# A ring of three x blocks, loads of two blocks by 4 MB, and products copied straight to the output buffer in a kernel for pairwise feature products

## The chip, the cores and the metric

The kernel runs on one core of a Trainium2 chip. The metric is the device time of one execution in microseconds (us). Each kernel was executed several times; the text gives the median of the fast runs with their lowest and highest value. A ratio is the mean time of one kernel's fast runs over the mean of the other's in the same rounds, so it is not quite the ratio of the two medians.

## The reference

```python
# r_inputs: (4096, 32, 64) float32, W: (496, 64, 64) float32; 496 = 32 * 31 / 2 pairs
idx_i, idx_j = np.triu_indices(F, k=1)
vi = inputs[:, idx_i, :]
vj = inputs[:, idx_j, :]
vidots = jnp.einsum('bpd,pde->bpe', vi, W)
return vidots * vj                      # (4096, 496, 64) float32, 520 MB
```

For every pair of features i < j, the 64 values of feature i are multiplied by a 64 x 64 matrix, and the result is multiplied elementwise by feature j. The result is 520 MB; inputs and weights are 42 MB.

## The kernel before

The batch is cut into 32 tiles of 128 rows, one row per partition; two tiles make a block of x (2 MB). Per tile, TensorE (PE) transposes (turns) x and multiplies it by the turned weights into PSUM, the memory that holds its results; a step is up to 16 pairs. VectorE multiplies the step by feature j into an output buffer. For some steps ScalarE copies the PSUM result to a temporary, and GpSimd multiplies that into the output buffer. A tile has five output groups (90 to 105 pairs, about 3 MB each), and three output buffers rotate. Each full group goes out by one transfer from the SyncE queue.

```python
xpool = ctx.enter_context(tc.tile_pool(name="xpool", bufs=2))   # two blocks of x, a tile each
tpool = ctx.enter_context(tc.tile_pool(name="tpool", bufs=4))   # temporaries, and reordered W
opool = ctx.enter_context(tc.tile_pool(name="opool", bufs=3))   # output groups
...
LATE = 6
loads = {place[blk * NB, LATE]: blk + 1 for blk in range(2, NBLK - 1)}   # one 2 MB load per block
...
        if i in aside and c0 == 0 and s not in no_aside:
            tmp = tpool.tile([P, CH, 2, E2], F32, tag="tmp", name=f"tmp_{s}")
            nc.scalar.copy(tmp, src)
            nc.gpsimd.tensor_mul(dst, tmp, xj)
        else:
            nc.vector.tensor_mul(dst, src, xj)
```

At the start, W comes in four chunks. Each is reordered by copies (`order_w`, into `rp`), then turned by PE. The copies of the last chunk are written at step 54 and 55 of the program.

Of the kernel before, what the change touches and what calls it, by code (L numbers as in the profile page):

```python
# [8 lines left out]
F32 = mybir.dt.float32  # L9
# [3 lines left out]
def kernel(  # L13
# [16 lines left out]
    nc = tc.nc  # L30

    B, F, D = x.shape
    P = 128
    NB = 2
    assert 2 * D == P and B % (NB * P) == 0
    NBLK = B // (NB * P)
    NP = F * (F - 1) // 2
    E2 = D // 2
    BANK = 512
    CH = BANK // E2  # L40
    RUN = 2 * BANK // P
# [7 lines left out]
    aside = (1, 3, 5, 7, 9, 11, 13)  # L49
# [2 lines left out]
    wrows = list(zip(cuts[:-1], cuts[1:]))  # L52

    const = ctx.enter_context(tc.tile_pool(name="const", bufs=1))
    xpool = ctx.enter_context(tc.tile_pool(name="xpool", bufs=2))
    xtpool = ctx.enter_context(tc.tile_pool(name="xtpool", bufs=4))
    tpool = ctx.enter_context(tc.tile_pool(name="tpool", bufs=4))
    opool = ctx.enter_context(tc.tile_pool(name="opool", bufs=3))
    psum = ctx.enter_context(tc.tile_pool(name="psum", bufs=4, space=bass.MemoryType.PSUM))

    ident = const.tile([P, P], F32, tag="ident", name="ident")
    make_identity(nc, ident)

    xs = {}

    def rows_of(dram: bass.AP, blk: int) -> bass.AP:
        return dram[blk * NB * P : (blk + 1) * NB * P]

    def new_x(blk: int):

        xs[blk] = xpool.tile([P, 1 + NB * F, D], F32, tag="xs", name=f"xs_{blk}")
        nc.gpsimd.memset(xs[blk][:, 0, :], 0.0)  # L72

    def load_x(blk: int, eng, k0: int = 0, k1: int = NB):
        src = rows_of(x, blk).rearrange("(p k) f d -> p (k f) d", k=NB)
        eng.dma_start(out=xs[blk][:, 1 + k0 * F : 1 + k1 * F, :], in_=src[:, k0 * F : k1 * F, :])  # L76


    wflat = w.rearrange("p d e -> p (d e)")
# [1 line left out]
    EU = 2 * BANK // P  # L81
    NU = E2 // EU

    def load_w(c: int, eng=nc.sync):

        a, b = wrows[c]
        pool, tag = ((opool, "ot"), (opool, "ot"), (const, "w3"), (const, "w3"))[c]
        raw[c] = pool.tile([P, D * D], F32, tag=tag, name=f"raw_{c}")
        eng.dma_start(out=raw[c][: b - a, :], in_=wflat[a:b])

    def order_w(c: int, k: int, copy):
        r = wrows[c][1] - wrows[c][0]
        rp = tpool.tile([P, EU, 2, D], F32, tag="tmp", name=f"rp_{c}_{k}")
        src = raw[c][:r, :].rearrange("p (d h e) -> p e h d", h=2, d=D)
        copy(rp[:r], src[:, k * EU : (k + 1) * EU])  # L95
        return rp

    def turn_w(c: int, k: int, rp, copy):
        r = wrows[c][1] - wrows[c][0]
        if c not in wT:  # L100
            wT[c] = const.tile([P, r, E2], F32, tag=f"w{c}", name=f"wT_{c}")
        pt = psum.tile([P, EU, P], F32, tag="ps", name=f"ptw_{c}_{k}")
        for n in range(EU):
            nc.tensor.transpose(  # L104
                pt[:, n, :r], rp[:r, n].rearrange("p h d -> p (h d)"), ident[:r, :r]
            )
        copy(wT[c][:, :, k * EU : (k + 1) * EU], pt[:, :, :r].rearrange("p e r -> p r e"))  # L107

    def turn_x(blk: int, k: int, q: int, copy):

        pt = psum.tile([P, RUN, P], F32, tag="ps", name=f"ptx_{blk}_{k}_{q}")
        for n in range(RUN):
            s = k * F + q * RUN + n
            nc.tensor.transpose(  # L114
                pt[:, n, :], xs[blk][:, s : s + 2, :].rearrange("p f d -> p (f d)"), ident
            )
        xT = xtpool.tile([P, RUN, P], F32, tag="xT", name=f"xT_{blk}_{k}_{q}")
        copy(xT, pt)  # L118
        return xT
# [16 lines left out]
    LEAD = 3  # L136
# [5 lines left out]
    place = {ts: n for n, ts in enumerate(sched)}  # L142
# [8 lines left out]
    for c, orders, turns in (  # L151
# [4 lines left out]
        for k in range(NU):  # L156
            due.setdefault(orders[k], []).append(("order", c, k))
            due.setdefault(turns[k], []).append(("turn", c, k))
    no_aside = range(52, 67)
    LATE = 6  # L160
    loads = {place[blk * NB, LATE]: blk + 1 for blk in range(2, NBLK - 1)}
    loads[place[LEAD, LATE]] = 2

    new_x(0)
    load_x(0, nc.sync, 0, 1)
    load_w(0)
    load_w(1)
    load_x(0, nc.sync, 1, NB)
    load_w(2)
    new_x(1)  # L170
    load_x(1, nc.sync)

    v, p, a = nc.vector.tensor_copy, nc.gpsimd.tensor_copy, nc.scalar.copy
    xT, rps = {}, {}
    xT[0, 0, 0] = turn_x(0, 0, 0, a)
    due[0] = [d for d in due[0] if d != ("x", 0, 0, 0)]
    for k, copy in enumerate((v, v, v, a)):
        rps[0, k] = order_w(0, k, copy)
# [4 lines left out]
    for s, (t, st) in enumerate(sched):  # L183
        blk, kt = divmod(t, NB)
        g, i, c0, m = steps[st]
        if s in loads:
            new_x(loads[s])
            load_x(loads[s], nc.scalar)
        for what, *args in due.get(s, ()):
            if what == "x":  # L190
                xT[tuple(args)] = turn_x(*args, a)
            elif what == "turn":
                turn_w(*args, rps.pop(tuple(args)), a)
            else:
                c, k = args
                rps[c, k] = order_w(c, k, (v, v, p, v)[c] if k % 2 == 0 else (v, v, p, a)[c])
                if (c, k) == (2, NU - 1):
                    load_w(3, nc.scalar)

        base, end = groups[g]  # L200
        pa = p0[i] + c0
        if pa == base:
            ots[t] = opool.tile([P, cap, D], F32, tag="ot", name=f"ot_{t}_{g}")
        ot = ots[t]
        ps = psum.tile([P, 2, CH, E2], F32, tag="ps", name=f"ps_{s}")
        for c, (lo, hi) in enumerate(wrows):
            lo, hi = max(pa, lo), min(pa + m, hi)
            if lo < hi:
                for h in range(2):
                    n = i + 1 - h  # L210
                    nc.tensor.matmul(  # L211
                        ps[:, h, lo - pa : hi - pa, :],
                        xT[blk, kt, n // RUN][h * D : (h + 1) * D, n % RUN, :],
                        wT[c][h * D : (h + 1) * D, lo - wrows[c][0] : hi - wrows[c][0], :],
                        start=True,
                        stop=True,
                    )
        o = pa - base
        j = 1 + kt * F + i + 1 + c0
        dst = ot[:, o : o + m, :].rearrange("p m (h e) -> p m h e", h=2)  # L220
        src = ps[:, :, :m, :].rearrange("p h m e -> p m h e")
        xj = xs[blk][:, j : j + m, :].rearrange("p m (h e) -> p m h e", h=2)
        if i in aside and c0 == 0 and s not in no_aside:
            tmp = tpool.tile([P, CH, 2, E2], F32, tag="tmp", name=f"tmp_{s}")
            nc.scalar.copy(tmp, src)  # L225
            nc.gpsimd.tensor_mul(dst, tmp, xj)  # L226
        else:
            nc.vector.tensor_mul(dst, src, xj)  # L228

        ends = (p0[2], end) if s < NS and (t, g) == (0, 0) else (end,)  # L230
        if pa + m in ends:
            n0 = p0[2] if len(ends) > 1 and pa + m == end else base
            nc.sync.dma_start(  # L233
                out=rows_of(out, blk).rearrange("(p k) n d -> p k n d", k=NB)[:, kt, n0 : pa + m, :],
                in_=ot[:, n0 - base : pa + m - base, :],
            )
# [27 lines left out]
```

## Time and profile before

| | before |
|---|---|
| time, median (lowest to highest) | 1354.63 us (1353.6 to 1355.21, 4 runs beside the changed kernel) |
| span of the profiled run | 1353.3 us |
| busy: PE, VectorE, GpSimd, ScalarE | 87%, 71%, 39%, 28% |
| rate of HBM (the chip's main memory) over the span | 415 GB/s |
| output transfers / loads of x in the steady part | 160 of about 3 MB / 14 of 2 MB |

The lines that the prediction quotes are not shown again. Two more lines of the same page belong to them: the clock of PE and the bytes moved, in 40 equal slices of the span (one digit, or one number in GB/s, each). They are flat, apart from the start and the end: no place in the kernel moves fewer bytes than its neighbours, and the clock hardly dips (0.948 over the span). With the transfers holding the DMA engines for 98% of the span, I read this as the transfers setting the pace everywhere.

```profile
PEclk9989999989999898999989999899998999989997
...
GB/s 386 370 426 408 424 427 431 428 432 431 418 414 419 433 412 418 422 413 426 428 407 422 417 425 410 423 421 407 425 410 426 419 422 427 401 432 428 415 417 319
```

### The profile page before, as it was taken

The page shows a single profiled execution, that of the slowest core. Times are in us where ns is not written, and L with a number is a line of the kernel's source. Part 1 is how long each engine was busy: PE and PEld are TensorE (multiplying, and loading weights), DVE is VectorE, ACT ScalarE, POOL GpSimd, SP SyncE. Part 2 cuts the span into 40 slices and gives each one's busy share as a digit, 9 for nine tenths or more (in the row PEclk, how much of TensorE's full clock was granted, in tenths as well). Part 3 has the DMA queues.
Part 4 walks back from the last instruction along what each step waited for, and adds up shares of the span by engine and source line. Part 5 has one row for each costly group of instructions (what it writes and reads, how often), then busy time and mean ns, then how long its engine had stood idle before and what let it go on. Part 6 is the DMA issues. An engine that isn't in the chain of part 4 may idle for free.

```text
span 1353.3 us, 17856 instructions
## 1 busy us (share of the span) xinstructions
PE 1180.3 (87%) x7424; PEld 690.9 (51%) x7424; DVE 956.9 (71%) x1262; ACT 374.1 (28%) x367; POOL 530.2 (39%) x246
## 2 busy tenths in 40 slices
PE   6989889889799897988879989888987989988994
PEld 4556545545455454555445545454554545545552
DVE  5778768767677676776757777676775767767774
ACT  3432222222232232222222222222222222223221
POOL 1813424444243443433444334433434434344431
PEclk9989999989999898999989999899998999989997
DMA  9999999999999999999999999999999999999997
GB/s 386 370 426 408 424 427 431 428 432 431 418 414 419 433 412 418 422 413 426 428 407 422 417 425 410 423 421 407 425 410 426 419 422 427 401 432 428 415 417 319
DMA packets 26273, 562.92 MB, mean 416 GB/s; under 512 B 2912, under 2 KB 2912, under 8 KB 3040
## 3 DMA queue, kind: packets, MB, share of 16 engines
q1 hardware_dynamic: 24048, 530.59, 92.4%
q10 hardware_dynamic: 2144, 31.20, 5.5%
q8 instruction: 58, 0.95, 0.3%
q14 instruction: 23, 0.19, 0.0%
HBM read 41.68 MB, written 520.09 MB: 415 GB/s over the span
## 4 chain that ended last, share of the span: by engine, by line
DMA 50%; PE 25%; DVE 17%; POOL 3%; issue 2%; ACT 0%; DVEq 0%; SPq 0%; POOLq 0%; ACTq 0%
DMA out_dram<-ot 50%; PE ps L211 20%; DVE ot L228 17%; PE ptx L114 4%; POOL ot L226 3%; PE ptw L104 1%; DMA raw<-in_L_rec_W_dram 1%; ACT tmp L225 0%; DVE rp L95 0%; POOL rp L95 0%; DVEq L228 0%; ACT wT L107 0%; SPq L76 0%; POOLq L226 0%; SPq L233 0%
## 5 line engine op out<-in xcount | busy, mean ns | idle before, releaser
L228 DVE TENSOR_TENSOR ot<-ps,xs 128x1024 f32<-128x1024 f32 (+15 forms) x1252 | 945.6, 808 | 364.7 <-DMA out_dram<-ot 185.9
L211 PE MATMUL ps<-wT,xT 64*128 64x512 f32 (+13 forms) x6272 | 1034.9, 473 | 132.8 <-DVE ot L228 121.3
L211 PEld LDWEIGHTS ps<-wT,xT 64*128 64x128 f32 x6272 | 563.7, 197 | 569.9 <-DVE ot L228 306.8
L226 POOL TENSOR_TENSOR ot<-tmp,xs 128x1024 f32<-128x1024 f32 x220 | 519.6, 2362 | 647.4 <-ACT tmp L225 457.1
L225 ACT COPY tmp<-ps 128x1024 f32<-128x1024 f32 x220 | 222.7, 1012 | 500.1 <-PE ps L211 459.6
L118 ACT COPY xT<-ptx 128x1024 f32<-128x1024 f32 x128 | 129.6, 1012 | 428.2 <-PE ptx L114 428.2
L114 PE MATMUL ptx<-ident,xs 128*128 128x128 f32 x1024 | 141.2, 281 | 18.5 <-DVE ot L228 9.9
L114 PEld LDWEIGHTS ptx<-ident,xs 128*128 128x128 f32 x1024 | 111.0, 142 | 64.3 <-issue 44.1
L72 POOL MEMSET xs<- 128x64 f32 x16 | 2.4, 152 | 148.6 <-DVE ot L228 148.6
L104 PE MATMUL ptw<-ident,rp 128*128 128x128 f32 (+1 forms) x128 | 19.2, 305 | 3.9 <-DVE rp L95 3.9
L104 PEld LDWEIGHTS ptw<-ident,rp 128*128 128x128 f32 (+1 forms) x128 | 16.2, 160 | 10.3 <-DVE rp L95 5.0
L107 ACT COPY wT<-ptw 128x1024 f32<-128x1024 f32 (+1 forms) x15 | 14.8, 984 | 21.4 <-PE ptw L104 21.4
L95 DVE COPY rp<-raw 128x1024 f32<-128x1024 f32 (+1 forms) x9 | 10.7, 1219 | 11.1 <-DMA raw<-in_L_rec_W_dram 11.1
L95 POOL COPY rp<-raw 128x1024 f32<-128x1024 f32 x4 | 8.0, 1994 | 0.1
L95 ACT COPY rp<-raw 112x1024 f32<-112x1024 f32 (+1 forms) x3 | 5.9, 1959 | 5.1 <-POOL ot L226 3.3
L107 DVE COPY wT<-ptw 128x1024 f32<-128x1024 f32 x1 | 1.2, 1224 | 3.3 <-PE ptw L104 3.3
L118 ACT ACT_TABLE_LOAD x1 | 1.3, 1283 | 0.7 <-PEq L251 0.7
masks.py:197 POOL MEMSET ident<- 128x128 f32 x1 | 0.2, 206 | 0.3 <-POOLq L251 0.3
masks.py:199 POOL TENSOR_SCALAR_AFFINE_SELECT ident<-ident 128x128 f32<-128x128 f32 x1 | 0.3, 295 | 0.0
L251 POOL MEMSET const-float32-0.0<- 128x1 f32 x1 | 0.1, 99 | 0.2 <-issue 0.2
L251 POOL MEMSET const-bfloat16-1.0<- 128x1 bf16 x1 | 0.1, 102 | 0.0
L251 POOL MEMSET const-uint8-127<- 128x1 uint8 x1 | 0.1, 102 | 0.0
(1 smaller groups left out, 0.1 us busy)
## 6 DMA issues: line engine op xcount, KB each, us to landing
out_dram<-ot SPq DMA_DIRECT2D x64, 3360.0 KB, 16.2
out_dram<-ot SPq DMA_DIRECT2D x32, 3168.0 KB, 15.4
out_dram<-ot SPq DMA_DIRECT2D x32, 3104.0 KB, 17.0
out_dram<-ot SPq DMA_DIRECT2D x31, 2880.0 KB, 16.4
xs<-in_r_inputs_dram ACTq DMA_DIRECT2D x14, 2048.0 KB, 16.6
raw<-in_L_rec_W_dram SPq DMA_DIRECT2D x3, 2048.0 KB, 14.3
xs<-in_r_inputs_dram SPq DMA_DIRECT2D x2, 1024.0 KB, 10.9
xs<-in_r_inputs_dram SPq DMA_DIRECT2D x1, 2048.0 KB, 24.6
```

Source lines behind the costliest of these rows:

```text
L72: nc.gpsimd.memset(xs[blk][:, 0, :], 0.0)
L95: copy(rp[:r], src[:, k * EU : (k + 1) * EU])
L104: nc.tensor.transpose(pt[:, n, :r], rp[:r, n].rearrange("p h d -> p (h d)"), ident[:r, :r])
L107: copy(wT[c][:, :, k * EU : (k + 1) * EU], pt[:, :, :r].rearrange("p e r -> p r e"))
L114: nc.tensor.transpose(pt[:, n, :], xs[blk][:, s : s + 2, :].rearrange("p f d -> p (f d)"), ident)
L118: copy(xT, pt)
L211: nc.tensor.matmul(ps[:, h, lo - pa : hi - pa, :], xT[blk, kt, n // RUN][h * D : (h + 1) * D, n % RUN, :], wT[c][h * D : (h + 1) * D, lo - ...
L225: nc.scalar.copy(tmp, src)
L226: nc.gpsimd.tensor_mul(dst, tmp, xj)
L228: nc.vector.tensor_mul(dst, src, xj)
L251: nc = _bacc.Bacc("TRN2", target_bir_lowering=False, num_devices=1)
```

## The change

The intent: fewer and larger loads, no temporary between ScalarE and GpSimd, no repeated zeroing of a guard column. x lives in one array of three slots. A load brings two blocks of x by one 4 MB transfer. ScalarE copies its product to the output buffer, and GpSimd multiplies it there in place. The reordered W uses a part of the third slot that x does not need yet.

```diff
-    xpool = ctx.enter_context(tc.tile_pool(name="xpool", bufs=2))
-    tpool = ctx.enter_context(tc.tile_pool(name="tpool", bufs=4))
 ...
+    NX = 3
+    xs = const.tile([P, 1 + NX * NB * F, D], F32, tag="xs", name="xs")
+    nc.gpsimd.memset(xs[:, 0, :], 0.0)
+
+    def slot(blk: int, k: int, i: int = 0) -> int:
+        b = blk % 2 * (1 + blk // 2 % 2)
+        return 1 + (b * NB + k) * F + i
 ...
+    def load_two(blk: int, eng):
+        n = NB * F
+        dst = xs[:, 1:, :].rearrange("p (b n) d -> p b (n d)", n=n)
+        step = (slot(blk + 1, 0) - slot(blk, 0)) // n
+        src = x[blk * NB * P : (blk + 2) * NB * P].rearrange("(b p k) f d -> p b (k f d)", b=2, k=NB)
+        eng.dma_start(out=dst[:, 0 : step + 1 : step, :], in_=src)
 ...
-        rp = tpool.tile([P, EU, 2, D], F32, tag="tmp", name=f"rp_{c}_{k}")
+        rp = xs[:, 1 + (NX - 1) * NB * F :, :].rearrange("p (n e h) d -> p n e h d", e=EU, h=2)[:, k]
 ...
-    no_aside = range(52, 67)
 ...
-    loads = {place[blk * NB, LATE]: blk + 1 for blk in range(2, NBLK - 1)}
-    loads[place[LEAD, LATE]] = 2
+    loads = {place[LEAD, LATE]: 2}
+    for blk in range(3, NBLK - 1, 2):
+        loads[place[blk * NB, LATE]] = blk + 1
 ...
-        if i in aside and c0 == 0 and s not in no_aside:
-            tmp = tpool.tile([P, CH, 2, E2], F32, tag="tmp", name=f"tmp_{s}")
-            nc.scalar.copy(tmp, src)
-            nc.gpsimd.tensor_mul(dst, tmp, xj)
+        if i in aside and c0 == 0:
+            nc.scalar.copy(dst, src)
+            nc.gpsimd.tensor_mul(dst, dst, xj)
```

By `slot`, even blocks always lie in slot 0 and odd blocks in slots 1 and 2 in turn. So a pair goes to slots 0 and 1, or to slots 0 and 2, and in the second case block 1 (5, 9, 13), at work in slot 1, lies between.

More of the change, by code (lines that the diff above doesn't have):

```diff
@@ L62 @@
     make_identity(nc, ident)
-    xs = {}
+    NX = 3
[4 more added lines that the diff above has]
+        return 1 + (b * NB + k) * F + i
     def rows_of(dram: bass.AP, blk: int) -> bass.AP:
         return dram[blk * NB * P : (blk + 1) * NB * P]
-    def new_x(blk: int):
-        xs[blk] = xpool.tile([P, 1 + NB * F, D], F32, tag="xs", name=f"xs_{blk}")
-        nc.gpsimd.memset(xs[blk][:, 0, :], 0.0)
     def load_x(blk: int, eng, k0: int = 0, k1: int = NB):
         src = rows_of(x, blk).rearrange("(p k) f d -> p (k f) d", k=NB)
-        eng.dma_start(out=xs[blk][:, 1 + k0 * F : 1 + k1 * F, :], in_=src[:, k0 * F : k1 * F, :])
+        eng.dma_start(
+            out=xs[:, slot(blk, k0) : slot(blk, k1 - 1) + F, :], in_=src[:, k0 * F : k1 * F, :]
+        )
+    def load_two(blk: int, eng):
[4 more added lines that the diff above has]
+        eng.dma_start(out=dst[:, 0 : step + 1 : step, :], in_=src)
     wflat = w.rearrange("p d e -> p (d e)")
@@ L112, in turn_x @@
         for n in range(RUN):
-            s = k * F + q * RUN + n
+            s = slot(blk, k, q * RUN + n) - 1
             nc.tensor.transpose(
-                pt[:, n, :], xs[blk][:, s : s + 2, :].rearrange("p f d -> p (f d)"), ident
+                pt[:, n, :], xs[:, s : s + 2, :].rearrange("p f d -> p (f d)"), ident
             )
@@ L158 @@
             due.setdefault(turns[k], []).append(("turn", c, k))
-    no_aside = range(52, 67)
     LATE = 6
-    loads = {place[blk * NB, LATE]: blk + 1 for blk in range(2, NBLK - 1)}
-    loads[place[LEAD, LATE]] = 2
-    new_x(0)
+    loads = {place[LEAD, LATE]: 2}
+    for blk in range(3, NBLK - 1, 2):
+        loads[place[blk * NB, LATE]] = blk + 1
     load_x(0, nc.sync, 0, 1)
@@ L169 @@
     load_w(2)
-    new_x(1)
     load_x(1, nc.sync)
@@ L186 @@
         if s in loads:
-            new_x(loads[s])
-            load_x(loads[s], nc.scalar)
+            load_two(loads[s], nc.scalar)
         for what, *args in due.get(s, ()):
@@ L218 @@
         o = pa - base
-        j = 1 + kt * F + i + 1 + c0
+        j = slot(blk, kt, i + 1 + c0)
         dst = ot[:, o : o + m, :].rearrange("p m (h e) -> p m h e", h=2)
         src = ps[:, :, :m, :].rearrange("p h m e -> p m h e")
-        xj = xs[blk][:, j : j + m, :].rearrange("p m (h e) -> p m h e", h=2)
-        if i in aside and c0 == 0 and s not in no_aside:
-            tmp = tpool.tile([P, CH, 2, E2], F32, tag="tmp", name=f"tmp_{s}")
-            nc.scalar.copy(tmp, src)
-            nc.gpsimd.tensor_mul(dst, tmp, xj)
+        xj = xs[:, j : j + m, :].rearrange("p m (h e) -> p m h e", h=2)
+        if i in aside and c0 == 0:
+            nc.scalar.copy(dst, src)
+            nc.gpsimd.tensor_mul(dst, dst, xj)
         else:
```

## The prediction

> **What bounds the kernel now.** I read the page first: the slices, the DMA queues and the chain of waits.
>
> ```profile
> DMA  9999999999999999999999999999999999999997
> ...
> q1 hardware_dynamic: 24048, 530.59, 92.4%
> q10 hardware_dynamic: 2144, 31.20, 5.5%
> q8 instruction: 58, 0.95, 0.3%
> ...
> HBM read 41.68 MB, written 520.09 MB: 415 GB/s over the span
> ...
> DMA 50%; PE 25%; DVE 17%; POOL 3%; issue 2%; ACT 0%; DVEq 0%; SPq 0%; POOLq 0%; ACTq 0%
> ```
>
> The transfers hold the 16 DMA engines for 98% of the span, while the busiest engine that computes, PE, stands at 87%. The totals of waits say the same: VectorE and GpSimd stop because an output buffer is still on its way to HBM.
>
> ```profile
> DVE ot L228 <- DMA out_dram<-ot: 185.9, 84, 5.8
> ...
> POOL ot L226 <- DMA out_dram<-ot: 153.1, 59, 5.5
> ...
> POOL xs L72 <- DVE ot L228: 148.6, 14, 18.3
> ...
> ACT tmp L225 <- POOL ot L226: 36.1, 9, 5.0
> ```
>
> I then went to the single packets of the trace. A packet of an output row (26880 bytes, one partition) takes 0.996 us, one of 23040 bytes 0.855 us, one of 16384 bytes of x 0.611 us. One engine's sixteenth of all data adds up to about 1304 us. The last completion lands at 1351.6 us. The rest is the q8 line[...]. If they fall to one engine, (1351.6 - 1304) / 58 = 0.8 us each. The completion marks fit this: between the first and the last engine to finish one output transfer lie 2 us at 190 us and, away from loads, 6 to 7 us from 450 us on. So the end is set by one DMA engine that never idles: after 120 us, each output transfer is issued at least 3.7 us, and from 210 us on at least 6.7 us, before the previous one has fully landed. The kernel can only become faster by some idle time in the first 125 us, and only slower if the output queue runs dry.
>
> [...] 16 x 26880 / 0.996 = 432 GB/s. [...] a 2 MB load is 8 packets per engine; taken in turn with 8 output packets it needs 8 x (0.611 + 0.996) = 12.9 us, and with about 2 us to start and finish on the first engine, more on the last, that is the 16.6 us of the issues below (count, size, us to landing). [...] after 4.7 us without work the stretch of 40 matmuls took 7.99 us, after 2.1 us 7.04. [...]
>
> ```profile
> 700.64 7.99 PE ps L211 x40
> ...
> 739.61 7.04 PE ps L211 x40
> ```
>
> ```profile
> xs<-in_r_inputs_dram ACTq DMA_DIRECT2D x14, 2048.0 KB, 16.6
> ```
>
> **The change, part by part.** (1) 15 of 16 memsets of 152 ns go: 2.3 us of GpSimd, beside other work; worth 0. GpSimd's 148.6 us of waiting before them delays nothing that sets the end.
>
> (2) The products go to the output buffer directly. ScalarE loses its wait for a free temporary (36.1 us), but now waits for the landing of the output buffer, which GpSimd waited for anyway (153.1 us). The 1012 ns copy then falls after the landing instead of ahead of it. The group's end is later by at most about 1 us, inside a lead of 6.7 us: worth 0. The exception that kept steps 52 to 66 on VectorE goes too; those lie at about 70 to 95 us. Idle DMA time after the start is 2.5 us in 25 to 50 us, 0.8 in 50 to 75 and 1.6 in 100 to 125 (mean over the engines). I count -1 us.
>
> (3) Seven loads of 4 MB replace 14 of 2 MB. The bytes and packets are the same. A fixed cost saved is beside the transfers: worth 0.
>
> (4) What decides it is in the program order of the changed kernel. The ring puts blocks 4 and 5 (8 and 9, 12 and 13) into slots 0 and 1, which are neighbours, but blocks 2 and 3 (6 and 7, 10 and 11, 14 and 15) into slots 0 and 2, with a step of two over slot 1, in which the block at work lies. For these four loads the build takes the whole stretch as written. Each waits for the products of the first output group (90 pairs) of the tile at work, and the next product on VectorE and on GpSimd, which read slot 1, wait for the load. The three contiguous loads have neither wait. So four times nothing is multiplied from the load's issue to its landing, while the output queue empties.
>
> What one such stall costs the slowest DMA engine, in steady state, from the moment L at which the load is issued and the 90-pair transfer goes out:
> - Work queued at L: before a tile's last output goes out, 7.5 us are left of the previous one (the lead at such an issue where no load is near). 6.3 us later (679.29 to 685.61 in the issue times) 1.2 us of that are left, then 8 x 0.996 = 8.0 and 8 x 0.855 = 6.8: 16.0 us.
> - The load: 16 packets x 0.611 = 9.8 us, and one instruction fetch, 0.8 us. Taken in turn, both queues end together, at L + 26.6. It lands 0.5 us later.
> - From landing to the next output: the same group after a wait in the kernel before:
>
> ```profile
> 689.29 3.83 DVE L228 TENSOR_TENSOR ot<-ps,xs 128x768 f32<-128x768 f32 x4 [3.74 <-DMA out_dram<-ot]
> ...
> 692.62 2.35 POOL L226 TENSOR_TENSOR ot<-tmp,xs 128x1024 f32<-128x1024 f32 x1 [0.97 <-ACT tmp L225]
> ```
>
> The landing was at 689.17, the output was issued at 695.00: 5.8 us, of which the line shows the chain: a product frees a PSUM buffer, PE fills it, ScalarE copies, GpSimd multiplies. After more than 20 us without work PE is at half clock; I choose 0.5 us for it.
> - From issue to running packets: 0.85 us, twice seen where the queue was nearly dry (at 35.83 and 103.63 us).
>
> Idle: 0.5 + 5.8 + 0.5 + 0.85 = 7.7 us. Afterwards the outputs come at intervals of about 7.8, 8.3, 6.5, 7.0 us against transfers of 7.5, 8.0, 8.0, 6.8 plus the fetches, so the queue is near empty for a tile; I choose 0.3 us for gaps. That makes 8 us. In the first of the four, at about 150 us, the queue is shorter (about 11 us) and drains before the load ends too: also 8. Four stalls: 32 us. Sum: 1354.8 + 32 - 1 = 1386 us, 2.3% more.
>
> **The rivals.** (a) The outputs queued cover the stalls: within 2%. For it speaks that each load shares the engines with outputs, so neither runs dry early; against it that the three outputs in the ring are all that is queued, and 16.0 us is no more than what passes during 16 load packets. Each microsecond more in the queue at L takes one off each stall: with 2 more, 1378. (b) All is hidden, DMA is the bound and its bytes are the same: 1354. That would need the load not to wait for the group at work: issued 6.3 us earlier it would leave 6.3 us more behind it, and the cost would be near 1 us each. The waits in the program speak against it. (c) ScalarE, now tied to the output buffers, or GpSimd becomes the bound: GpSimd is busy 39%, ScalarE 28%; even 1 us for each of 160 outputs disappears in the lead. If it did not, I would see some 1400 us or more. (d) The start gains from removed temporaries: at most the 4.9 us of idle above, so 1350 without the stalls.
>
> **Range and chances.** 1381.9 us is the 2% border, 4 us below my number. Stalls of 5 to 10 us give 1374 to 1394. Slower by over 2%: 0.66; within 2%: 0.33; faster: 0.01.
>
> **What would show it.** In the changed profile: four waits of VectorE for the load of x, each of 20 to 27 us, near 155, 435, 770 and 1110 us; in the slices DMA share and GB/s falling in four places and nowhere else; 4 MB loads landing in 24 to 29 us; the chain of waits passing through the load of x for some 7%; q8 still 58 packets; GpSimd's product still 2.36 us in place. It is wrong if VectorE's waits for the load are short, if the queue never dries, or if output transfers are issued late outside these four places.

## The result, and the profile after

The changed kernel took 1396.83 us (1395.98 to 1396.99, 4 runs) against 1354.63: ratio 1.0311, 95% interval 1.0293 to 1.0329. It is slower, as predicted, but by 42 us in place of 31, and outside of the range (1374 to 1394).

The page of the changed kernel, the lines that answer to those of the prediction and of the section above: clock, DMA share and GB/s by slices, the queues (q1 carries the output, q10 the loads that ScalarE issues, q8 instructions), HBM, and the chain by engine and by line.

```profile
PEclk9899889989999699998999969999899988999997
DMA  9899979999999699999999969999999996999997
GB/s 379 320 412 429 409 317 426 429 418 430 431 422 422 248 430 427 428 423 426 431 428 422 410 266 428 429 429 418 431 430 421 419 407 261 427 430 428 429 431 339
...
q1 hardware_dynamic: 24048, 530.59, 89.6%
q10 hardware_dynamic: 2032, 31.20, 5.3%
q8 instruction: 58, 0.95, 0.2%
...
HBM read 41.68 MB, written 520.09 MB: 403 GB/s over the span
...
DMA 54%; PE 23%; DVE 16%; POOL 2%; issue 2%; ACT 2%; DVEq 0%; SPq 0%; ACTq 0%; POOLq 0%
DMA out_dram<-ot 45%; PE ps L219 18%; DVE ot L235 16%; DMA xs<-in_r_inputs_dram 7%; PE ptx L125 4%; POOL ot L233 2%; DMA raw<-in_L_rec_W_dram 2%; ACT ot L232 1%; PE ptw L115 1%; POOL xs L106 1%; ACT xT L129 0%; DVE xs L106 0%; DVEq L235 0%;
```

The bytes are those of before. The GB/s fall to 317, 248, 266 and 261 in four slices, and the clock of PE falls with them, to 0.6 in the second and third and 0.8 in the last; one more dip (320) is in the second slice, which the prediction had not expected to be deeper than before (370). The load of x has entered the chain with 7% of the span.

The totals of waits (total us, times, longest) and the issues of the loads (count, size, median us to landing, that is, to the last completion mark):

```profile
ACT ot L232 <- DMA out_dram<-ot: 271.4, 67, 8.0
...
POOL ot L233 <- DMA xs<-in_r_inputs_dram: 101.4, 4, 26.3
DVE ot L235 <- DMA xs<-in_r_inputs_dram: 99.7, 4, 25.9
DVE xs L106 <- DMA raw<-in_L_rec_W_dram: 19.8, 2, 11.2
```

```profile
xs<-in_r_inputs_dram ACTq DMA_DIRECT2D x7, 4096.0 KB, 25.7
```

Four waits of VectorE and GpSimd for a load of x are new, 25 us each on the mean. The waits for a landed output, which before belonged to GpSimd, now belong to ScalarE. The last of the four lines is the second surprise: VectorE waits twice for a chunk of W, and in the kernel before once (11.1 us).

**One stall.** The load was issued at 452.77 us and landed at 478.45. The windows around it; the columns are the stretch and its length, each engine's busy time and count of instructions, granted clock, DMA share, GB/s:

```profile
core 0: us, PE busy (x) PEld busy (x) DVE busy (x) ACT busy (x) POOL busy (x), PEclk, DMA share, GB/s
453.00:465.00 12.00, 2.09 (x18) 1.29 (x14) 0.00 (x0) 2.02 (x2) 0.00 (x0) 0.72 1.01 406
465.00:478.50 13.50, 0.00 (x0) 0.00 (x0) 0.00 (x0) 0.00 (x0) 0.00 (x0) 0.50 0.59 248
478.50:486.00 7.50, 6.41 (x20) 3.29 (x22) 5.23 (x6) 1.01 (x1) 4.71 (x2) 0.52 0.00 0
486.00:495.00 9.00, 9.00 (x70) 5.58 (x66) 6.73 (x10) 4.05 (x4) 7.09 (x3) 1.00 0.96 406
```

First the engines stand and the transfers go on; then the engines work and nothing is transferred. In the third row 0 GB/s are moved while PE works at a mean granted clock of 0.52. The timeline of the restart (start, length, engine, tile, idle time before it and what ended that):

```profile
478.57 2.89 DVE L235 TENSOR_TENSOR ot<-ps,xs 128x768 f32<-128x768 f32 x3 [25.89 <-DMA xs<-in_r_inputs_dram]
...
479.59 8.88 PE L219 MATMUL ps<-wT,xT 64*128 64x512 f32 x34 [23.44 <-DVE ot L235]
...
481.71 1.01 ACT L232 COPY ot<-ps 128x1024 f32<-128x1024 f32 x1 [24.46 <-PE ps L219]
...
482.80 2.35 POOL L233 TENSOR_TENSOR ot<-ot,xs 128x1024 f32<-128x1024 f32 x1 [1.83 <-ACT ot L232]
...
484.48 1.89 DVE L235 TENSOR_TENSOR ot<-ps,xs 128x1024 f32<-128x1024 f32 x2 [0.88 <-PE ps L219]
485.77 0.33 SPq L240 DMA_DIRECT2D out_dram<-ot  x1
```

The same group in the kernel before, after a wait of 3.7 us:

```profile
690.30 5.69 PE L211 MATMUL ps<-wT,xT 64*128 64x512 f32 x28 [2.42 <-DVE ot L228]
...
691.53 1.01 ACT L225 COPY tmp<-ps 128x1024 f32<-128x1024 f32 x1 [2.60 <-PE ps L211]
...
695.00 0.33 SPq L233 DMA_DIRECT2D out_dram<-ot  x1
```

From VectorE's first product (478.57, before 689.29) ScalarE's copy starts after 3.14 us in place of 2.24, and the output is issued after 7.20 us in place of 5.71. Before, GpSimd's product came last (end at 694.97). After, it is VectorE's, which waited 0.88 us for PE.

**The start.** Windows of 50 to 62 us, first after, then before:

```profile
50.00:62.00 12.00, 5.30 (x16) 3.08 (x18) 4.91 (x5) 2.87 (x2) 0.53 (x1) 0.59 0.63 259
```

```profile
50.00:62.00 12.00, 12.00 (x80) 7.32 (x78) 8.25 (x9) 6.20 (x7) 10.85 (x5) 1.00 0.99 361
```

VectorE's timeline there says why, in the changed kernel:

```profile
44.84 0.96 DVE L235 TENSOR_TENSOR ot<-ps,xs 128x768 f32<-128x768 f32 x1 [1.19 <-POOL ot L233]
54.39 1.03 DVE L106 COPY xs<-raw 112x1024 f32<-112x1024 f32 x1 [8.60 <-DMA raw<-in_L_rec_W_dram]
```

The copy that reorders the last chunk of W (112 rows) stands among the products of the first tile's second output group and waits 8.60 us for its chunk. In the trace it is the 25th instruction that VectorE executes; in that of the kernel before it is the 47th, at 75.64 us. PE, whose PSUM buffers VectorE does not free, stands too (busy for 5.30 of the 12 us), and no output is ready.

**Where the 42 us lie.** I lined up the same output transfers of the two runs by the time of their last landing, at places where both kernels had loaded equally much. The changed kernel is later by 15.2 us after the first stall, 24.5 after the second, 33.6 after the third and 42.2 after the fourth, and by nothing more from there on. So stalls two to four cost 9.3, 9.1 and 8.6 us, and the start with the first stall 15.2.

### The profile page after: what moved, and what is told of

It is laid out like the page before. It is cut to its first block, busy times and chain, and to the rows that moved or that the text cites. A ratio compares the mean times of both kernels' runs of the same rounds, so it can differ in the third digit from the quotient of the medians.

```text
span 1395.1 us, 17912 instructions
## 1 busy us (share of the span) xinstructions
PE 1145.0 (82%) x7424; PEld 673.5 (48%) x7424; DVE 948.2 (68%) x1258; ACT 377.8 (27%) x371; POOL 537.9 (39%) x235
## 4 chain that ended last, share of the span: by engine, by line
DMA 54%; PE 23%; DVE 16%; POOL 2%; issue 2%; ACT 2%; DVEq 0%; SPq 0%; ACTq 0%; POOLq 0%
DMA out_dram<-ot 45%; PE ps L219 18%; DVE ot L235 16%; DMA xs<-in_r_inputs_dram 7%; PE ptx L125 4%; POOL ot L233 2%; DMA raw<-in_L_rec_W_dram 2%; ACT ot L232 1%; PE ptw L115 1%; POOL xs L106 1%; ACT xT L129 0%; DVE xs L106 0%; DVEq L235 0%; SPq L78 0%; SPq L240 0%
## 5 line engine op out<-in xcount | busy, mean ns | idle before, releaser
L219 PE MATMUL ps<-wT,xT 64*128 64x512 f32 (+13 forms) x6272 | 995.6, 460 | 160.6 <-DVE ot L235 148.9
L233 POOL TENSOR_TENSOR ot<-ot,xs 128x1024 f32<-128x1024 f32 x224 | 529.3, 2363 | 828.6 <-ACT ot L232 711.8
L219 PEld LDWEIGHTS ps<-wT,xT 64*128 64x128 f32 x6272 | 544.4, 190 | 576.7 <-DVE ot L235 301.6
L232 ACT COPY ot<-ps 128x1024 f32<-128x1024 f32 x224 | 226.9, 1013 | 579.0 <-PE ps L219 301.7
L115 PE MATMUL ptw<-ident,xs 128*128 128x128 f32 (+1 forms) x128 | 20.0, 315 | 13.0 <-DVE ot L235 9.1
L115 PEld LDWEIGHTS ptw<-ident,xs 128*128 128x128 f32 (+1 forms) x128 | 16.9, 165 | 19.2 <-issue 14.2
L106 DVE COPY xs<-raw 128x1024 f32<-128x1024 f32 (+1 forms) x9 | 9.1, 1042 | 19.8 <-DMA raw<-in_L_rec_W_dram 19.8
L106 POOL COPY xs<-raw 128x1024 f32<-128x1024 f32 x4 | 8.0, 2022 | 1.6 <-PE ptw L115 1.6
L106 ACT COPY xs<-raw 112x1024 f32<-112x1024 f32 (+1 forms) x3 | 6.0, 1988 | 1.8 <-DMA raw<-in_L_rec_W_dram 1.8
## 6 DMA issues: line engine op xcount, KB each, us to landing
out_dram<-ot SPq DMA_DIRECT2D x32, 3168.0 KB, 16.5
xs<-in_r_inputs_dram ACTq DMA_DIRECT2D x7, 4096.0 KB, 25.7
```

The source lines that it names most:

```text
L106: copy(rp[:r], src[:, k * EU : (k + 1) * EU])
L115: nc.tensor.transpose(pt[:, n, :r], rp[:r, n].rearrange("p h d -> p (h d)"), ident[:r, :r])
L219: nc.tensor.matmul(ps[:, h, lo - pa : hi - pa, :], xT[blk, kt, n // RUN][h * D : (h + 1) * D, n % RUN, :], wT[c][h * D : (h + 1) * D, lo - ...
L232: nc.scalar.copy(dst, src)
L233: nc.gpsimd.tensor_mul(dst, dst, xj)
```

## The experiments

The theory after reading the traces: two causes, the four loads that step over a slot in use (9 us each, 36 together) and the moved copies of W at the start (6 us). Rivals: that 4 MB loads, or the copy straight to the output buffer, cost something by themselves.

**e1_two_loads**, each pair of blocks by two loads of 2 MB, so that no load steps over a slot:

```diff
-            load_two(loads[s], nc.scalar)
+            load_x(loads[s], nc.scalar)
+            load_x(loads[s] + 1, nc.scalar)
```

> The changed kernel with each 4 MB load made as two 2 MB loads, one for each slot, so that no load steps over the slot at work. Theory (the step over the slot at work makes products and load wait for each other, four times about 9 us; the rest, about 6 us, is lost at the start): 1396.8 - 36 = 1361 us, no wait of VectorE for a load of x after the start, four dips of the DMA share gone. Rival (the ring itself, or ScalarE's copy to the output buffer, costs something at every output): the time stays above 1380.

Measured: 1361.05 us (1360.1 to 1362.52), ratio 1.0051 (1.0036 to 1.0066). 35.8 of the 42.2 us are gone with the stepping loads, and VectorE and GpSimd no longer wait for any load of x (nor do they in e2).

**e2_middle_slot**, the loads stay at 4 MB, but even blocks lie in the middle slot, so that both kinds of pair are neighbours (one more zero column, and blocks 0 and 1 of four swap their place in memory):

```diff
-        b = blk % 2 * (1 + blk // 2 % 2)
-        return 1 + (b * NB + k) * F + i
+        b = (1, 0, 1, 2)[blk % 4]
+        return 1 + (b > 0) + b * SL + k * F + i
+    def dram_block(blk: int) -> int:
+        return blk + (1, -1, 0, 0)[blk % 4]
```

> One 4 MB load for two blocks is kept, but even blocks take the middle slot, so that each pair fills two neighbouring slots and the slot at work is never stepped over. Theory: as e1, 1361 us. Rival (a load of 4 MB itself holds up the outputs for too long, 26 us against 16): stays near 1390, while e1 is fast.

Measured: 1363.33 us (1362.19 to 1364.09), ratio 1.0066 (1.0051 to 1.0081). The dips in the middle have gone, with 4 MB loads; the one at the start (the second digit) is left:

```profile
DMA  9899999999999999999999999999999999999997
```

So it is the step, not the size of the load. The 2.3 us above e1 may be a small cost of the larger loads or of the other layout; these runs do not tell which (e5 below lies 2.7 us above e4 in the same way).

**e3_w_in_place**, the copies of the last chunk of W are held at their place in the program:

```diff
-        copy(rp[:r], src[:, k * EU : (k + 1) * EU])
+        ins = copy(rp[:r], src[:, k * EU : (k + 1) * EU])
+        if c == 3:
+            tc.keep_in_program_order(ins)
```

> The changed kernel, with the copies that reorder the fourth chunk of W held at their place in the program, so that VectorE does not sit in one of them for 8.6 us at 46 us while that chunk is still loading. Theory: 6 us less, 1391 us, the four dips stay, the output that was issued at 62.0 us goes out at about 51. Rival (the start lost its time to ScalarE's copies, which now wait for output buffers): stays at 1397.

Measured: 1390.54 us (1389.32 to 1391.34), ratio 1.027 (1.0253 to 1.0287). 6.3 us come back: the start. The output that went out at 62.0 us in the changed kernel goes out at 49.7.

**e4_both**, e1 and e3 together:

> e1 and e3 together. Theory: the two costs add up and nothing else is left: 1355 us, the same as before. Rival (a further cost of the direct copy or of the ring): 1360 or more remains.

Measured: 1355.81 us (1355.49 to 1356.06), ratio 1.0012 (0.9997 to 1.0026). The two causes add up, and with both removed the kernel before and the changed one take the same time.

**e8_direct_only**, the kernel before with nothing but the direct copy:

```diff
-            tmp = tpool.tile([P, CH, 2, E2], F32, tag="tmp", name=f"tmp_{s}")
-            nc.scalar.copy(tmp, src)
-            nc.gpsimd.tensor_mul(dst, tmp, xj)
+            nc.scalar.copy(dst, src)
+            nc.gpsimd.tensor_mul(dst, dst, xj)
```

> The kernel before with one part of the change alone: ScalarE copies to the output buffer and GpSimd multiplies there; two blocks of x, 2 MB loads, the exception for the steps 52 to 66 and the temporaries for W stay. The build moves VectorE's copy of the fourth chunk of W forward here too. Theory: only the start is lost, 1354.6 + 6 = 1361 us, no waits for x. Rival (the copy's wait for the output buffer costs at every output): 1370 or more, spread over the whole span. Rival (the direct copy gains at the start): below 1353.

Measured: 1360.17 us (1359.25 to 1360.58), ratio 1.0042 (1.0027 to 1.0057). The direct copy, the main part of what the prediction had counted as a gain of 1 us, costs 5.6 (the exception for steps 52 to 66 is still in place here).

**e12_direct_w_in_place**, e8 with the copies of W held as in e3:

> The kernel before with the direct copy into the output buffer alone, and the reordering copies of the fourth chunk of W held at their place in the program. The direct copy alone cost 5.6 us (1360.2); its trace shows VectorE waiting 8.6 us for that chunk, as in the changed kernel. If the moved copies are all of it, the time is that of the kernel before, 1353.5 to 1356 us; if the later copy of ScalarE costs something in steady state, it stays at 1358 to 1361 us.

Measured: 1354.95 us (1354.67 to 1355.14), ratio 1.0 (0.9983 to 1.0017). VectorE's waits for chunks of W, in e8 and in e12:

```profile
DVE rp L95 <- DMA raw<-in_L_rec_W_dram: 19.3, 2, 10.8
```

```profile
DVE rp L95 <- DMA raw<-in_L_rec_W_dram: 11.3, 1, 11.3
```

The direct copy itself costs nothing that these runs can tell; the prediction's account, that ScalarE's later copy fits in the lead of the output queue, agrees with this. The whole cost of e8 was that, with the temporaries no longer used for products, the W copies moved forward in VectorE's order (the first is its 25th instruction in e8 too, and its 51st in e12).

**e6_half_strided**, the stepping loads carry half of each row (2 MB, 8 KB per partition and block); the other half follows 14 steps later by two contiguous loads:

```diff
+            dst = xs[:, 1:, :].rearrange("p (b n) d -> p b n d", n=n)[:, 0:3:2, :F, :]...
+            eng.dma_start(out=dst, in_=src[:, :, 0, :])
...
+            for b in (late, late + 1):
+                tc.keep_in_program_order(load_x(b, nc.scalar, 1, NB))
```

> The changed kernel, but the four strided loads carry only half the rows (2 MB); the other half comes 14 steps later by contiguous loads. VectorE still waits for each strided load, for about 14 to 16 us in place of 25. If what a stall costs is the time in which the output queue is empty: 16.0 us are queued, 8 packets of each queue are taken in turn, so some 6 to 7 us of outputs are left at the landing against 7 to 8 us until the next output runs: at most 1 to 2 us each, 1396.8 - 4 x 7.5 = about 1367 (1361 to 1370). If it is the time in which nothing is multiplied: half the cost stays, about 1379.

Measured: 1398.55 us (1397.7 to 1398.82), ratio 1.0325 (1.031 to 1.034). A miss: half the bytes, and nothing saved. The load did land sooner (20.8 us against 25.6), but the output queue ended sooner with it. The packets of the changed kernel show how the two share an engine. At the end of the stall at 478 us one engine is still at work (start to end in us, size in bytes, queue; q10 is x, q1 output):

```
474.46 - 475.31  23040  q1
475.31 - 475.92  16384  q10
475.92 - 476.77  23040  q1
476.77 - 477.38  16384  q10
477.38 - 477.99  16384  q10
```

In these lines the two queues change after one packet, be it of 23040 bytes (0.85 us) or of 16384 (0.61 us), as long as output is left. An engine has 16 packets of the load. Of output, 184 packets ended between the issue and the landing, 11.5 for each of 16 engines; the engine that is late had some 16 (an estimate: 25.2 us from the issue to its last packet, less 16 x 0.61 us for the load, at 0.95 us each). There both end together, whether the load's packets are of 16 KB or of 8 KB: in the changed kernel and in e6 no output is left at the landing (table below). e6 had halved the packets' size and kept their number. What is left of a stall is the bare restart: the time from the end of both queues to the next output packet.

**e9_half_rows**, **e10_every_2nd_row**, **e11_every_4th_row**: fewer packets instead. The stepping load carries the lower 64 partitions, every second or every fourth partition alone; the others follow 14 steps later.

```diff
-        eng.dma_start(out=dst[:, 0 : step + 1 : step, :], in_=src)
+        r = P // step                                                    # e9: 64 for the stepping loads
+        eng.dma_start(out=dst[:r, 0 : step + 1 : step, :], in_=src[:r])
+        r = 2 if step > 1 else 1                                         # e10 (e11: 4)
+        eng.dma_start(out=dst[::r, 0 : step + 1 : step, :], in_=src[::r])
```

> As the changed kernel, but the four strided loads carry the rows of 64 partitions alone (2 MB, 8 packets of 16 KB for each DMA engine); the rows of the other 64 follow 14 steps later in two contiguous loads of 1 MB. The run that halved the strided load by halving each packet (2 MB, 16 packets of 8 KB) saved nothing: its stalls were as dear as before. Theory, formed from that miss: load and output queue are served packet by packet in turn, the output queue holds some 16 packets per engine when the load is issued, so 16 load packets end with the last output packet whatever their size, and the restart of 8 to 9 us is bare idle time; 8 load packets end when 8 output packets (about 7 us) are left, which cover most of the restart. Then the load lands in some 14 to 17 us in place of 25.7, stalls two to four cost 0 to 3 us each in place of 9, the first, with a shorter queue, 2 to 5, and with the 6 us of the start the time is 1364 to 1374 us. Rival: the cost of a stall is the wait as such, whatever the load's packets: 1390 to 1398 us.

Measured: 1408.84 us (1407.88 to 1409.79), ratio 1.0399 (1.0384 to 1.0415). A miss again, and for another reason, which e10 shows.

> As the run before it with half the rows, but the strided loads carry every second partition (64 of 128) in place of the lower 64; the others follow 14 steps later. In that run the load also had 8 packets per engine and the bare idle time in a stall did fall (slowest engine: from 8.6 us to 4.9 us by the packets in flight), but every packet that ran beside a 64-partition load was slower (16 KB took 0.74 to 0.78 us on the mean in place of 0.58, 313 GB/s during the load in place of 420), which cost more than was saved. If it is the lower half of the partitions that makes packets slow, here they keep their pace: load lands 16 to 18 us after its issue, some 4 to 6 us of output are left then, each stall costs 3 to 5 us in place of 9, time 1372 to 1386 us. If any load of 64 partitions is slow: 1400 to 1410. If the stall costs the same whatever the packets: 1394 to 1398.

Measured: 1387.55 us (1386.44 to 1389.13), ratio 1.0246 (1.0228 to 1.0263), 1.6 us above the stretch given.

> Every fourth partition in the strided loads: 1 MB, 4 packets of 16 KB per engine; the other three quarters follow 14 steps later as six contiguous loads of 0.5 MB. By packets in turn the load lands 11 to 13 us after its issue with 8 us or more of output left, which cover the restart: stalls two to four cost 0 to 2 us, the first 0 to 4, time 1361 to 1370 us if packets keep their pace. If the stall costs the same whatever the packets: 1394 to 1398. If loads of few partitions slow all packets: above 1390 with little idle time, to be told by packet times.

Measured: 1380.32 us (1379.05 to 1381.94), ratio 1.0189 (1.0174 to 1.0204; whether that is over 2% is unclear). 10 us above the stretch given.

The waits of VectorE for the load, in e10 and in e11:

```profile
DVE ot L241 <- DMA xs<-in_r_inputs_dram: 67.2, 4, 16.9
```

```profile
DVE ot L241 <- DMA xs<-in_r_inputs_dram: 50.7, 4, 12.8
```

From the packets of the five traces, for stalls two to four. "Left" is the output still queued at the landing, to its last packet's end; "restart" runs from the last packet of x to the first packet of the next output; "bare" is the time without any packet of data:

| kernel | load, packets per engine | landed after | left | restart | bare |
|---|---|---|---|---|---|
| changed | 16 of 16 KB | 25.6 to 25.7 us | 0 | 8.3 to 8.7 us | 8.3 to 8.7 us |
| e6 | 16 of 8 KB | 20.8 to 20.9 | 0 | 8.2 to 8.6 | 8.2 to 8.6 |
| e9 | 8 of 16 KB | 19.1 to 19.6 | 2.9 to 3.3 | 8.0 to 9.2 | 4.3 to 5.1 |
| e10 | 8 of 16 KB | 16.6 | 3.8 | 8.3 to 9.3 | 3.8 to 4.4 |
| e11 | 4 of 16 KB | 12.4 to 12.5 | 5.5 to 5.6 | 8.9 to 9.4 | 2.1 to 2.5 |

The restart hardly differs among the five. What a stall costs is the restart less what is left in the queue when the load lands, and that depends on the number of the load's packets. In the first stall the queue is shorter, and little was saved: 8.1 us bare in the changed kernel, 8.6 in e10 and 7.0 in e11. e10 should have saved (8.5 - 4.2) x 3 = 13 us by this and saved 9; e11 (8.5 - 2.3) x 3 + 1.1 = 20 and saved 16.5; e6 should have saved nothing and lost 1.7. The 2 to 4 us that are missing I put down to the split itself, with its later small loads; this was not tested. For e11, 8 us or more of output had been expected to be left at the landing, and 5.5 were; the load's first packet ran 4.7 us after its issue (in the changed kernel 3.6 to 3.7).

e9 and e10 have the same packets and bytes. Windows of 10 us within the second stall, while the load runs, e9 first:

```profile
464.00:474.00 10.00, 0.00 (x0) 0.00 (x0) 0.00 (x0) 0.00 (x0) 0.00 (x0) 0.50 1.04 344
```

```profile
456.00:466.00 10.00, 0.00 (x0) 0.00 (x0) 0.00 (x0) 0.00 (x0) 0.00 (x0) 0.50 0.92 392
```

With the engines fully busy (DMA share 1.04) e9 moves 344 GB/s. Its packets are slower: in these windows 16 KB took 0.87 us on the mean and an output packet of 23040 bytes 1.00 us, in e10 0.61 and 0.88 us. (The 0.74 to 0.78 and 0.58 us in the expectation of e10 come out of the traces only if the completion marks of 4 bytes are counted with the packets; without them they are 0.83 to 0.88 and 0.61 us.) In e10 and e11 16 KB took 0.61 us, as in loads of all 128 partitions. So the same bytes in the same number of packets were slower to the lower 64 partitions than to every second one. The cause of that was not shown. Added up over the run, the packets of x took 91.4 us of all 16 engines in e9 against 76.9 in e10, and those of q1 1254.3 against 1249.1: 20 of the 21 us by which e9 is above e10.

**e7_before_120**, on the prediction's claim of a single late engine: the kernel before with the last output group of every fifth tile split into a transfer of 120 rows and one of 8.

```diff
+            cut = (120, P) if g == len(groups) - 1 and t % 5 == 4 else (P,)
+            for q0, q1 in zip((0, *cut), cut):
+                nc.sync.dma_start(out=...[q0:q1, kt, n0 : pa + m, :], in_=ot[q0:q1, ...])
```

> The kernel before, with every fifth tile's last output (six of them) sent as 120 partitions and 8 partitions. If one DMA engine is late because PE's instructions are fetched by it, and if it is the engine that a transfer of 120 partitions leaves out, it carries 6 x 8 us less: 1354.6 - 30 to - 45 = 1310 to 1325. If the late engine is another of those that the 8 rows fall to, up to 6 us more; otherwise the same, 1355.

Measured: 1398.18 us (1381.45 to 1401.45, three fast runs; the fourth took 1417.73), ratio 1.0379 (1.031 to 1.0449). Inconclusive: from 8 us before to 25 us after the issue of each of the six split transfers, output packets took 1.16 to 1.23 us on the mean and single ones 4.0 to 5.5 us, against a mean of 0.95 in the kernel before. So the edit brought a larger disturbance than the one it was to measure. (Its q1 has 42 packets more, 24090: six times 15 + 8 completion marks in place of 16. That agrees with a transfer of 120 rows that leaves out one engine, as the expectation assumes.)

**e5_middle_and_w**, e2 and e3 together: 4 MB loads without either cause.

> Both causes removed with the 4 MB loads kept: even blocks in the middle slot of the ring (every pair of blocks goes to neighbouring slots, no load steps over one in use), and the reordering copies of the fourth chunk of W held at their place in the program. If start (6 us) and stalls (36 us) are all that the change costs, 1356 to 1358 us, within 0.3% of the kernel before; if 4 MB loads cost something of their own, 1362 or more. A gain over the kernel before (under 1352) is expected by no theory.

Measured: 1358.48 us (1356.84 to 1359.06), ratio 1.0024 (1.0007 to 1.004). All but 3.9 us of the loss is gone, and there is no gain. The time lies between the stretch given for no cost of 4 MB loads (to 1358) and the one given for such a cost (from 1362). No version beats the kernel before.

## Why the prediction was right or wrong

**The direction and the main mechanism were right.** Exactly the four stepping loads stall VectorE and GpSimd, the three contiguous ones do not; the stepping loads land in 25.6 to 25.7 us, but for the first (21.8), where 24 to 29 was said (the contiguous ones took 29.2 to 30.8); the load of x has 7% of the chain; q8 still has 58 packets; GpSimd's product in place takes 2.36 us. e1 and e2 remove the stalls and with them 35.8 and 33.5 us. The stalls came at 155, 453, 793 and 1133 us, the last three 18 to 23 us later than said. One of the prediction's own signs of being wrong was met too: an output was issued late outside the four places, at the start (62.0 us, in the kernel before 50.4).

**Step (2), "I count -1 us", failed.** The start cost 6 us. The prediction looked at the direct copy as work, and found that it fits in the lead of the queue. No run speaks against that (e12: ratio 1.0). It did not look at what else the temporaries had ordered: the copies of W's last chunk had shared their pool with the products. Once they did not, the first copy became VectorE's 25th instruction in place of its 47th, ahead of the products that follow, and waited 8.60 us for a load. The built order, which needs no run, shows the move (the expectation of e8 reads it there); I had looked there for the waits of the loads of x and not for moved copies. e3 and e8 with e12 show the cost from both sides: 6.3 and 5.6 us.

**Step (4) was right in kind, and one term was too small.** The cost of a stall was put at 8 us and was 9 (9.3, 9.1, 8.6). The term: "5.8 us" from landing to the next output and "I choose 0.5 us" for PE at half clock, 6.3 together. Measured, 7.0 to 7.4 us in stalls two to four (6.8 in the first). The other terms held: 0.45 us from the last packet to the landing (0.5 said), 0.83 us from issue to packets (0.85 said). The 5.8 us came from a restart after 2.4 us of idle PE, at a clock of 1.00: 26 matmuls filled 4.70 us. After 23 us of idle PE, in the second stall, the mean clock was 0.52 over the restart, and 20 matmuls filled 6.41 us. The four stalls point the same way: from landing to the next output took 6.84 and 6.98 us where the mean clock was 0.64 and 0.63, and 7.32 and 7.42 where it was 0.51 and 0.59. I take the clock to be the cause of the longer restart; a run that kept PE at work through the stall was not made, so this is argued and not shown. In the second stall the clock was 0.50 from 458.4 to 485.7 us, through nearly all of the restart, with gaps in PE's work. In the kernel before, in the prediction's own example, it fell to 0.50 in both stretches: for 6.8 us in the one after 4.7 us without work, and for 3.4 us in the one after only 2.1 us.

**The sum.** 36 for 32, and +6 for -1: 42 for 31. The start is the larger half of the error. With stalls of 9 us and the start as predicted the time would have been 1390 us, with stalls of 8 us and the start as measured 1393, both inside the range; it took both errors to leave it.

**Rival (a)** was refused rightly: the queue does dry up. The prediction's remark that each microsecond more in the queue takes one off each stall fits e10 and e11, from the other end: with 3.8 and 5.5 us left, the bare time fell by 4.3 and 6.2 us.

**The single late engine** is seen in the packets. In each of the last three stalls of the changed kernel only one packet at a time is still under way for the last 3.8 to 5.0 us before the queue is dry (from 474.0 to 478.0 us in the second), so one engine alone is at work; at the end of the kernel before, from 1347 to 1351 us. In the first stall it is 0.3 us. That the instruction fetches make it late was inferred, and stays so: e7 did not settle it. Nor do the traces number the engines.

## What to carry to other kernels

When a buffer is replaced by a ring, check for every load which slots its destination spans: here each load that stepped over a slot in use waited for the work on that slot and held it up (four waits of VectorE, 25 us each on the mean; none in e1 and e2), however well the bytes overlap. A stall behind a full transfer queue cost, here, about the restart time less what was still queued when it ended, and what was still queued went with the load's packets, not with its bytes: half the bytes in as many packets saved nothing (e6, 1398.55 us against 1396.83), half the packets, of every second partition, saved 9 us (e10, 1387.55). So count packets, not bytes. When a temporary goes, look in the built order for what its pool had been holding back, before running.
